# Bilinear pair products on one core: weight loads of eight pairs instead of four, and field 0 held in a store tile

## The chip, the cores and the metric

The kernel runs on one core of a Trainium2 chip. A core has five engines that run their own instruction streams: TensorE (PE) multiplies matrices, VectorE (DVE), ScalarE (ACT) and GpSimd (POOL) work element by element, SyncE (SP) here does nothing but issue DMAs. Sixteen DMA engines move the data between HBM and the on-chip memory (SBUF). The metric is device time in microseconds; the median of repeated runs counts.

## What is computed

The input holds 1024 samples of 32 fields with 128 numbers each; there is one 128 x 128 matrix for each of the 496 pairs of fields (i, j) with i < j. For each pair, field i goes through the pair's matrix, and the result is multiplied with field j element by element:

```python
v_i = inputs[:, I_IDX, :]                 # (1024, 496, 128)
v_j = inputs[:, J_IDX, :]
transformed = jnp.einsum('bpd,ped->bpe', v_i, W)   # W: (496, 128, 128)
return transformed * v_j                  # (1024, 496, 128), float32
```

The output alone is 260 MB; weights are 32.5 MB and fields 16.8 MB.

## The kernel before

Everything is transposed so that the 128 numbers of a field lie across the 128 partitions and the 1024 samples along the row. The pairs are walked from the highest i down, so that few fields are needed at the start: (30,31), (29,30), (29,31), (28,29) and so on. The unit of work, `u`, is half a pair (512 samples).

Sizes and pools, with what each slot costs in a partition's row:

```python
BT, HB = 1024, 512
WC = 2        # pairs per weight split
WL = 4        # pairs per weight load
OG = 2        # pairs per store
NATIVE = 5    # the first five fields go through PE as plain float32
LAG, WLEAD, XLEAD = 3, 4, 3
...
xpool = tile_pool(name="x", bufs=1)    # one tile of 4 KB for each of the 32 fields
spool = tile_pool(name="xs", bufs=2)   # split fields
rpool = tile_pool(name="wr", bufs=5)   # weights as loaded, WL * 512 B
wpool = tile_pool(name="ws", bufs=4)   # split weights
opool = tile_pool(name="o", bufs=4)    # store tiles, OG * 4 KB
ppool = tile_pool(name="ps", bufs=8)   # PSUM, one bank for each u
```

The loads. A weight load brings WL pairs; a row of it is WL * 512 B, one packet for each partition. On the host the weights are laid out so that each load is one contiguous block. All these DMAs, and the stores, go through the queue of SP, which takes them in order and waits there for whatever a DMA needs.

```python
def load_w(c, splits=(0, WL)):
    w_raw[c] = rpool.tile([P, WL, P], F32, tag="w")
    for a, b in zip(splits, splits[1:]):
        nc.sync.dma_start(out=w_raw[c][:, a:b, :], in_=wt[c, :, a:b, :])
```

After the first 15 pairs, PE works on split operands: ACT makes a rounded high part of each weight and each field, POOL the low part and a difference, and three fast matmuls with a scaling in between take the place of one slow float32 matmul.

```python
def split_w(c):                       # two pairs at once
    nc.scalar.mul(h, raw, 1.0 - 2.0**-13)
    nc.gpsimd.tensor_tensor(l, raw, h, ALU.subtract)
    nc.gpsimd.tensor_scalar(d, h, EPS, 1.0, ALU.mult, ALU.mult)
    nc.gpsimd.tensor_tensor(d, l, d, ALU.subtract)

def split_x(f, a):                    # half a field
    nc.scalar.mul(h, x_sb[f][:, s], 1.0 - 2.0**-13)
    nc.gpsimd.tensor_tensor(l, x_sb[f][:, s], h, ALU.subtract)
    nc.gpsimd.tensor_scalar(l, l, 1.0 / EPS, 1.0, ALU.mult, ALU.mult)
    nc.gpsimd.tensor_tensor(d, h, l, ALU.subtract)
```

A field is split when the one before it in the walk begins, half by half. Field 0 is only ever the left field of a pair: after its split nobody reads it.

```python
def first(u):                         # cut: the plain matmul of the first 15 pairs
    po[u] = ppool.tile([P, HB], F32)
    for t in (0, 1):
        nc.tensor.matmul(po[u], w_s[c][t][:, r], x_s[i][t][:, s], start=t == 0, stop=t == 1)
    nc.scalar.mul(po[u], po[u], 1.0 + EPS)

def second(u):
    nc.tensor.matmul(po[u], w_s[c][2][:, r], x_s[i][2][:, s], start=False, stop=True)
    if k == 0 and h == 0:
        ots[g] = opool.tile([P, OG, BT], F32, tag="ot")
    nc.vector.tensor_tensor(ots[g][:, k, s], po.pop(u), x_sb[j][:, s], ALU.mult)
    if k == OG - 1 and h == 1:        # cut: the last two pairs go out in quarters
        nc.sync.dma_start(out=out[g], in_=ots[g])
```

The walk:

```python
load_w(0, (0, 1, WL)); ...fields 30, 31, 29, 28; load_w(1); fields 27, 26; load_w(2); load_w(3)

for u in range(2 * NQ + LAG):
    q = u // 2
    if u % (2 * WL) == 0 and (q // WL + WLEAD) * WL < NQ:
        load_w(q // WL + WLEAD)
    if u < 2 * NQ:
        i, j = pairs[q]
        if u % 2 == 0 and j == i + 1 and 0 <= i - 2 - XLEAD:
            load_x(i - 2 - XLEAD)
        first(u)
    if u >= LAG:
        second(u - LAG)
    if u % 2 == 1:
        ...one of the splits that are due
```

Of the kernel before, what the change touches and what calls it, by code (L numbers as in the profile page):

```python
# [1 line left out]

# [4 lines left out]

F32 = mybir.dt.float32
F32R = mybir.dt.float32r
ALU = mybir.AluOpType  # L10

P = 128
NF = 32
NQ = NF * (NF - 1) // 2
BT = 1024
HB = 512
WC = 2
WL = 4
OG = 2
EPS = 2.0**-12  # L20
NATIVE = 5
LAG = 3
WLEAD = 4
XLEAD = 3


def _pairs():

    return [(i, j) for i in range(NF - 2, -1, -1) for j in range(i + 1, NF)]


@with_exitstack
def kernel(
    ctx: ExitStack,
    tc: tile.TileContext,
    xt: bass.AP,
    wt: bass.AP,
    out: bass.AP,
):

    nc = tc.nc
    pairs = _pairs()
    nchunk = NQ // WC

    xpool = ctx.enter_context(tc.tile_pool(name="x", bufs=1))  # L60
    spool = ctx.enter_context(tc.tile_pool(name="xs", bufs=2))
    rpool = ctx.enter_context(tc.tile_pool(name="wr", bufs=5))
    wpool = ctx.enter_context(tc.tile_pool(name="ws", bufs=4))
    opool = ctx.enter_context(tc.tile_pool(name="o", bufs=4))
    ppool = ctx.enter_context(tc.tile_pool(name="ps", bufs=8, space=bass.MemoryType.PSUM))

    x_sb = {}

    def load_x(f, n=1, pieces=1, eng=None):

        t = xpool.tile([P, n, BT], F32, tag=f"x{f}", name=f"x_{f}")
        s = BT // pieces
        for k in range(pieces):
            (eng or nc.sync).dma_start(out=t[:, :, k * s : (k + 1) * s], in_=xt[:, f : f + n, k * s : (k + 1) * s])  # L74
        for k in range(n):
            x_sb[f + k] = t[:, k, :]

    w_raw = {}

    def load_w(c, splits=(0, WL)):  # L80
        w_raw[c] = rpool.tile([P, WL, P], F32, tag="w", name=f"w_{c}")
        for a, b in zip(splits, splits[1:]):
            nc.sync.dma_start(out=w_raw[c][:, a:b, :], in_=wt[c, :, a:b, :])

    w_s = {}

    def split_w(c):

        k = c * WC % WL
        raw = w_raw[c * WC // WL][:, k : k + WC, :].rearrange("p q e -> p (q e)")  # L90
        h, l, d = [wpool.tile([P, WC * P], F32R, tag=t, name=f"{t}_{c}") for t in ("wh", "wl", "wd")]
        nc.scalar.mul(h, raw, 1.0 - 2.0**-13)  # L92
        nc.gpsimd.tensor_tensor(l, raw, h.bitcast(F32), ALU.subtract)  # L93
        nc.gpsimd.tensor_scalar(d, h.bitcast(F32), EPS, 1.0, ALU.mult, ALU.mult)  # L94
        nc.gpsimd.tensor_tensor(d, l.bitcast(F32), d.bitcast(F32), ALU.subtract)  # L95
        w_s[c] = (h, l, d)

    x_s = {}

    def split_x(f, a):  # L100

        if a == 0:
            x_s[f] = [spool.tile([P, BT], F32R, tag=t, name=f"{t}_{f}") for t in ("xh", "xl", "xd")]
        s = slice(a, a + HB)
        h, l, d = [t[:, s] for t in x_s[f]]
        nc.scalar.mul(h, x_sb[f][:, s], 1.0 - 2.0**-13)  # L106
        nc.gpsimd.tensor_tensor(l, x_sb[f][:, s], h.bitcast(F32), ALU.subtract)  # L107
        nc.gpsimd.tensor_scalar(l, l.bitcast(F32), 1.0 / EPS, 1.0, ALU.mult, ALU.mult)  # L108
        nc.gpsimd.tensor_tensor(d, h.bitcast(F32), l.bitcast(F32), ALU.subtract)  # L109

    nq0 = NATIVE * (NATIVE + 1) // 2
    c0 = nq0 // WC
    first_q = {i: q for q, (i, j) in reversed(list(enumerate(pairs)))}

    todo = []
    for c in range(c0, nchunk):
        todo.append(((c - 3) * WC + 1, max(c * WC, nq0), lambda c=c: split_w(c)))
    for i in range(NF - 2 - NATIVE, -1, -1):  # L120
        for a in range(0, BT, HB):
            todo.append((first_q[i + 1] + 1 if i < NF - 3 - NATIVE else 2, first_q[i], lambda i=i, a=a: split_x(i, a)))
    todo.sort(key=lambda t: t[1])

    load_w(0, (0, 1, WL))
    load_x(NF - 2, pieces=2, eng=nc.scalar)
    load_x(NF - 1, pieces=2, eng=nc.scalar)
    load_x(NF - 3)
    load_x(NF - 4)
    load_w(1)  # L130
    for f in range(NF - 5, NF - 4 - XLEAD, -1):
        load_x(f)
    load_w(2)
    load_w(3)


    ctx.enter_context(tc.manual_schedule())
    po, ots = {}, {}


    def first(u):
        q, h = divmod(u, 2)
        i, c = pairs[q][0], q // WC
        r = slice(q % WC * P, (q % WC + 1) * P)
        s = slice(h * HB, (h + 1) * HB)
        po[u] = ppool.tile([P, HB], F32, tag="po", name=f"po_{u}")
        if q < nq0:
            nc.tensor.matmul(po[u], w_raw[q // WL][:, q % WL, :], x_sb[i][:, s], start=True, stop=True)  # L148
        else:
# [5 lines that stand above are left out]
        q, h = divmod(u, 2)  # L155
        i, j = pairs[q]
        r = slice(q % WC * P, (q % WC + 1) * P)
        s = slice(h * HB, (h + 1) * HB)
        if q >= nq0:
            nc.tensor.matmul(  # L160
                po[u], w_s[q // WC][2][:, r], x_s[i][2][:, s], start=False, stop=True, skip_group_check=True
            )
        g, k = divmod(q, OG)
        if k == 0 and h == 0:
            ots[g] = opool.tile([P, OG, BT], F32, tag="ot", name=f"ot_{g}")
        nc.vector.tensor_tensor(ots[g][:, k, s], po.pop(u), x_sb[j][:, s], ALU.mult)  # L166
        if q >= NQ - 2:
            nc.sync.dma_start(out=out[g, :, k, s], in_=ots[g][:, k, s])
        elif k == OG - 1 and h == 1:
# [5 lines that stand above are left out]
            load_w(q // WL + WLEAD)  # L175
        if u < 2 * NQ:
            i, j = pairs[q]
            if u % 2 == 0 and j == i + 1 and 0 <= i - 2 - XLEAD:
                load_x(i - 2 - XLEAD)
            first(u)  # L180
        if u >= LAG:
            second(u - LAG)
        if u % 2 == 1:
            ready = [t for t in todo if t[0] <= q]
            if ready:
                ready[0][2]()
                todo.remove(ready[0])
    assert not todo


# [25 lines left out]
```

## Time and profile before

| | |
|---|---|
| time, median of 3 | 770.79 us (769.37 to 772.43) |
| span of the profiled execution | 769.2 us |
| PE, DVE, ACT, POOL busy | 93%, 81%, 82%, 80% |
| DMA | 310.11 MB, mean 403 GB/s |
| stores | 247 of 1024 KB, 8.9 us from issue to landing |
| weight loads | 123 of 256 KB and the first in two pieces, 9.1 us to landing |
| field loads | 30 of 512 KB and 4 of 256 KB |

How to read the profile: the page gives each engine's busy time and, in 40 slices of the span, tenths of it that were busy (9 is 90% or more); the row DMA is the mean of the sixteen DMA engines. Groups of instructions are named by line, engine and tile, written out<-in. A wait "DVE ot L166 <- DMA out_dram<-ot: 71.9, 84, 3.3" says that DVE, at its line 166, stood idle 71.9 us in total, 84 times, at most 3.3 us, until a store had landed. SPq is the DMA-issuing queue of SP. A store tile can be written again once its store has landed. Busy shares add up over stages with different limits, so a stage is read by itself.

### The profile page before, as it was taken

How to read it: one execution, taken by the hardware profiler on the slowest of the kernel's cores; microseconds unless marked ns; L12 is line 12 of the kernel's file. 1: busy time of each engine (PE TensorE's matmuls, PEld its weight loads, DVE VectorE, ACT ScalarE, POOL GpSimd, SP SyncE). 2: the span in 40 equal slices, each digit the busy share in tenths (PEclk: the TensorE clock that was granted, in tenths of full speed). 3: DMA queues.
4: the chain of work that ended last, by engine and by line, in shares of the span. 5: the costliest groups of instructions: out<-in, count | busy, mean ns of one | idle time of the engine just before them, and what ended most of it. 6: DMA issues, size and time to landing. Idle time of an engine off the chain costs nothing.

```text
span 769.2 us, 11797 instructions
## 1 busy us (share of the span) xinstructions
PE 715.0 (93%) x2946; PEld 548.9 (71%) x2946; DVE 625.3 (81%) x992; ACT 633.9 (82%) x1256; POOL 611.6 (80%) x883
## 2 busy tenths in 40 slices
PE   7989879889999898999998999999999999999994
PEld 3566657778777686776776877777777777777773
DVE  4767788888988787887787988888888888888885
ACT  2278878888888898898888989898889898998983
POOL 1988998998989878778778697878787869697660
PEclk9999999999999999999999999999999999999997
DMA  9899998999999999999999999999999999999997
GB/s 357 369 411 420 421 400 345 417 410 380 414 422 405 403 395 421 395 416 411 401 420 415 406 414 418 419 415 418 402 419 409 410 410 407 411 413 402 401 399 307
DMA packets 59108, 310.11 MB, mean 403 GB/s; under 512 B 6560, under 2 KB 6816, under 8 KB 27424
## 3 DMA queue, kind: packets, MB, share of 16 engines
q1 hardware_dynamic: 58464, 308.31, 98.8%
q10 hardware_dynamic: 576, 1.05, 0.4%
q8 instruction: 24, 0.39, 0.2%
q14 instruction: 44, 0.36, 0.1%
HBM read 49.28 MB, written 260.05 MB: 402 GB/s over the span
## 4 chain that ended last, share of the span: by engine, by line
PE 49%; DMA 32%; DVE 11%; POOL 6%; issue 1%; DVEq 0%; SPq 0%; ACT 0%; POOLq 0%
DMA out_dram<-ot 31%; PE po L151 31%; PE po L160 15%; DVE ot L166 11%; PE po L148 4%; POOL xd L109 2%; POOL wl L93 1%; POOL xl L107 1%; POOL wd L95 1%; POOL xl L108 0%; DMA x<-in_xt_dram 0%; POOL wd L94 0%; DVEq L166 0%; SPq L74 0%; ACT xh L106 0%
## 5 line engine op out<-in xcount | busy, mean ns | idle before, releaser
L166 DVE TENSOR_TENSOR ot<-po,x 128x512 f32<-128x512 f32 x992 | 625.3, 685 | 135.5 <-DMA out_dram<-ot 71.9
L152 ACT ACTIVATE po<-po 128x512 f32<-128x512 f32 x962 | 549.7, 583 | 109.7 <-PE po L151 61.4
L151 PE MATMUL po<-xh,wh 128*128 128x512 f32 x962 | 387.0, 402 | 25.0 <-DVE ot L166 23.9
L151 PE MATMUL po<-xl,wl 128*128 128x512 f32 x962 | 380.0, 395 | 14.6 <-POOL wl L93 14.1
L160 PE MATMUL po<-xd,wd 128*128 128x512 f32 x962 | 377.3, 393 | 0.0
L151 PEld LDWEIGHTS po<-xh,wh 128*128 128x128 f32 x962 | 181.5, 189 | 96.8 <-DVE ot L166 58.4
L93 POOL TENSOR_TENSOR wl<-w,wh 128x256 fp32r<-128x256 f32 x241 | 177.8, 738 | 74.2 <-ACT wh L92 74.2
L151 PEld LDWEIGHTS po<-xl,wl 128*128 128x128 f32 x962 | 181.9, 189 | 53.9 <-POOL wl L93 19.7
L160 PEld LDWEIGHTS po<-xd,wd 128*128 128x128 f32 x962 | 182.0, 189 | 39.0 <-ACT po L152 0.4
L95 POOL TENSOR_TENSOR wd<-wl,wd 128x256 fp32r<-128x256 f32 x241 | 177.8, 738 | 20.1
L94 POOL TENSOR_SCALAR wd<-wh 128x256 fp32r<-128x256 f32 x241 | 97.4, 404 | 20.3
L92 ACT ACTIVATE wh<-w 128x256 fp32r<-128x256 f32 x241 | 99.0, 412 | 0.0
L107 POOL TENSOR_TENSOR xl<-x,xh 128x512 fp32r<-128x512 f32 x52 | 67.2, 1292 | 17.0 <-ACT xh L106 17.0
L109 POOL TENSOR_TENSOR xd<-xh,xl 128x512 fp32r<-128x512 f32 x52 | 67.0, 1288 | 4.3
L106 ACT ACTIVATE xh<-x 128x512 fp32r<-128x512 f32 x52 | 32.5, 629 | 11.9 <-DMA x<-in_xt_dram 11.7
L108 POOL TENSOR_SCALAR xl<-xl 128x512 fp32r<-128x512 f32 x52 | 32.2, 620 | 4.6
L148 PE MATMUL po<-x,w 128*128 128x512 f32 x60 | 28.9, 647 | 3.9 <-DMA x<-in_xt_dram 3.9
L148 PEld LDWEIGHTS po<-x,w 128*128 128x128 f32 x60 | 12.3, 207 | 19.7 <-issue 15.1
L106 ACT ACT_TABLE_LOAD x1 | 1.3, 1283 | 2.6 <-issue 2.6
L203 POOL MEMSET const-float32-0.0<- 128x1 f32 x1 | 0.1, 98 | 0.2 <-issue 0.2
L203 POOL MEMSET const-bfloat16-1.0<- 128x1 bf16 x1 | 0.1, 101 | 0.0
L203 POOL MEMSET const-uint8-127<- 128x1 uint8 x1 | 0.1, 101 | 0.0
(1 smaller groups left out, 0.1 us busy)
## 6 DMA issues: line engine op xcount, KB each, us to landing
out_dram<-ot SPq DMA_DIRECT2D x247, 1024.0 KB, 8.9
w<-in_wt_dram SPq DMA_DIRECT2D x123, 256.0 KB, 9.1
x<-in_xt_dram SPq DMA_DIRECT2D x30, 512.0 KB, 9.2
x<-in_xt_dram ACTq DMA_DIRECT2D x4, 256.0 KB, 4.9
out_dram<-ot SPq DMA_DIRECT2D x4, 256.0 KB, 7.0
w<-in_wt_dram SPq DMA_DIRECT2D x1, 192.0 KB, 3.5
w<-in_wt_dram SPq DMA_DIRECT2D x1, 64.0 KB, 2.9
```

The costliest lines, as they stand in the source:

```text
L92: nc.scalar.mul(h, raw, 1.0 - 2.0**-13)
L93: nc.gpsimd.tensor_tensor(l, raw, h.bitcast(F32), ALU.subtract)
L94: nc.gpsimd.tensor_scalar(d, h.bitcast(F32), EPS, 1.0, ALU.mult, ALU.mult)
L95: nc.gpsimd.tensor_tensor(d, l.bitcast(F32), d.bitcast(F32), ALU.subtract)
L106: nc.scalar.mul(h, x_sb[f][:, s], 1.0 - 2.0**-13)
L107: nc.gpsimd.tensor_tensor(l, x_sb[f][:, s], h.bitcast(F32), ALU.subtract)
L109: nc.gpsimd.tensor_tensor(d, h.bitcast(F32), l.bitcast(F32), ALU.subtract)
L148: nc.tensor.matmul(po[u], w_raw[q // WL][:, q % WL, :], x_sb[i][:, s], start=True, stop=True)
L151: nc.tensor.matmul(po[u], w_s[c][t][:, r], x_s[i][t][:, s], start=t == 0, stop=t == 1)
L152: nc.scalar.mul(po[u], po[u], 1.0 + EPS)
L160: nc.tensor.matmul(po[u], w_s[q // WC][2][:, r], x_s[i][2][:, s], start=False, stop=True, skip_group_check=True)
L166: nc.vector.tensor_tensor(ots[g][:, k, s], po.pop(u), x_sb[j][:, s], ALU.mult)
```

## The change

A weight load brings eight pairs instead of four: half as many loads, and rows of 4 KB instead of 2 KB. Three buffers take the place of five, and the lead is two loads instead of four, the same sixteen pairs. The weight buffers grow from 5 x 2 KB to 3 x 4 KB in a partition. To make that room, field 0 loses its own tile of 4 KB: it is loaded late, six pairs before field 1 begins, into one of the four store tiles, and this tile goes back to the stores when field 0 has been split.

```diff
-WL = 4
+WL = 8
-WLEAD = 4
+WLEAD = 2
...
-    rpool = ctx.enter_context(tc.tile_pool(name="wr", bufs=5))
+    rpool = ctx.enter_context(tc.tile_pool(name="wr", bufs=3))
...
     def load_x(f, n=1, pieces=1, eng=None):
-        t = xpool.tile([P, n, BT], F32, tag=f"x{f}", name=f"x_{f}")
+        if f == 0:
+            t = opool.tile([P, OG, BT], F32, tag="ot", name="x_0")[:, :n, :]
+        else:
+            t = xpool.tile([P, n, BT], F32, tag=f"x{f}", name=f"x_{f}")
...
     for f in range(NF - 5, NF - 4 - XLEAD, -1):
         load_x(f)
-    load_w(2)
-    load_w(3)
...
-            if u % 2 == 0 and j == i + 1 and 0 <= i - 2 - XLEAD:
+            if u % 2 == 0 and j == i + 1 and 0 < i - 2 - XLEAD:
                 load_x(i - 2 - XLEAD)
+            if u == 2 * (first_q[1] - 6):
+                load_x(0)
             first(u)
```

Here `first_q[1]` is the place of the first pair of field 1, 435 of 496.

## The prediction

> **What bounds the kernel now.** I read the page from its slices down. The DMA row comes first, because the kernel moves 310 MB in 769 us.
>
> ```profile
> PE   7989879889999898999998999999999999999994
> POOL 1988998998989878778778697878787869697660
> DMA  9899998999999999999999999999999999999997
> DMA packets 59108, 310.11 MB, mean 403 GB/s; under 512 B 6560, under 2 KB 6816, under 8 KB 27424
> q1 hardware_dynamic: 58464, 308.31, 98.8%
> ```
>
> The 16 DMA engines are full in nearly every slice. PE shows nines too, but the windows (columns: PE, PEld, DVE, ACT, POOL busy, TensorE clock, DMA share, GB/s) show that it only follows:
>
> ```profile
> 16.00:120.00 104.00, 92.72 (x344) 65.68 (x343) 77.01 (x119) 70.54 (x144) 94.75 (x125) 0.97 0.98 399
> 120.00:240.00 120.00, 112.52 (x481) 90.40 (x479) 103.25 (x157) 105.02 (x213) 108.66 (x152) 0.99 1.00 404
> 240.00:480.00 240.00, 225.86 (x957) 176.25 (x958) 198.10 (x321) 208.29 (x415) 196.59 (x288) 1.00 1.01 409
> 480.00:740.00 260.00, 253.28 (x1069) 196.93 (x1069) 220.96 (x357) 232.32 (x457) 203.15 (x304) 1.00 1.01 411
> ```
>
> From 240 us on DMA is at its limit, while POOL is busy 203 of 260 us and DVE 221. A group of two pairs costs DVE 4 x 685 = 2.7 us; it arrives every 769/248 = 3.1 us. In the first stage POOL is busy 94.75 of 104 us (what is left is mostly the 0.05 to 0.08 us between its instructions): every new field brings a split, and the fields are still short. There, two things are near their limit at once.
>
> The waits say the same for the late stage (300 to 700 us):
>
> ```profile
> DVE ot L166 <- DMA out_dram<-ot: 43.8, 54, 2.5
> PEld po L151 <- DVE ot L166: 35.9, 69, 2.4
> PEld po L151 <- POOL wl L93: 3.6, 4, 0.9
> ```
>
> DVE waits for a store tile until its old store has landed; PE waits for DVE; hardly anyone waits for POOL. So from about 120 us on, a nanosecond of DMA time saved is saved, and a microsecond in which the DMA engines run dry is lost.
>
> **What one packet costs.** The trace records each DMA packet with size and duration. Grouped by size (median and mean ns):
>
> ```
> semaphore, 4 B    x6561    9    9
> weights, 2 KB    x16768   84   86   (1024 of them are pieces of fields 30, 31 and of the last stores)
> fields, 4 KB      x3840  159  173
> stores, 8 KB     x31666  309  317
> ```
>
> The medians lie on a line: 9 ns plus 75 ns for each 2 KB. All packets together take 12.25 million ns, 766 us on each of 16 engines, which is the span.
>
> **What the skill says.** "DMA: Bandwidth & Descriptors", section "Why small descriptors are slow (HBM only)", names a fixed overhead for each packet on the engine's internal bus and fixed metadata for each descriptor. The trace agrees in kind, with 9 ns; it is small beside 84. The same page, "Anatomy of one DMA — SWDGE (gpsimd) path", says that DMA engines don't wait on semaphores: the issuing sequencer does. That matters for the new wait below: SP's queue shows it, with 462.6 us of waiting for DVE ahead of stores. "Perfetto Trace Analysis", section "Identifying the Most-Contended Engine", warns that matmul busy time misleads about headroom. Agreed here: PE's 93% goes with 0.75 us of idle DVE in every 5.8 us around 660 us.
>
> **The change, part by part.**
>
> 1. *Weight packets.* Before, one load of four pairs puts 8 packets and one semaphore on each DMA engine: 8 x 84 + 9 = 681 ns, two loads 1362. After, one load of eight pairs is 8 x 159 + 9 = 1281. Saved: 81 ns for eight pairs, 62 x 81 = 5.0 us if everything counts. Loads issued before 120 us serve the stage in which POOL is as full as DMA. Pair 70 is then at work and loads run 16 pairs ahead, so those from pair 88 on count: 408/8 = 51 loads, 51 x 81 = 4.1 us. The mean of the fields' packets (173) is far over their median; those rows lie 128 KB apart in HBM, while a weight load is one contiguous block as before. I take the weights' excess as before, 2 to 5 ns, and book **-4.0 us**.
>
> 2. *Start.* Loads ahead of field 25 now hold 24 pairs of weights instead of 20: 256 KB more at about 410 GB/s is 0.6 us, less 0.2 for the better packets. POOL's chain begins when field 25 has landed and ACT has split it:
>
> ```profile
> ACT xh L106 <- DMA x<-in_xt_dram: 11.7, 1, 11.7
> POOL xl L107 <- ACT xh L106: 17.0, 3, 15.9
> ```
>
> After that POOL has no gap worth naming until 240 us (under 5 us in all between 17 and 240 us). **+0.4 us.**
>
> There is also something to win. At 25 us the SP queue stands still 8.8 us, because load w_7 waits for a weight split on POOL while two stores stand behind it; DMA runs dry for 1.7 + 0.8 us at 33.5 to 36.1 us.
>
> ```profile
> SPq L83 <- POOL wl L93: 8.8, 1, 8.8
> ```
>
> In the changed program the load in that place waits for PE alone, and the next one waits for an earlier split. That fills the hole. But a full POOL follows until after 100 us, where its results are ready only 1.6 us before DVE needs them, so I book 0.
>
> 3. *Field 0 in a store tile.* The load of field 0 now stands before pair 429. In the built program it takes the tile of store group 210, and from there three tiles rotate instead of four. The first DVE product of group 218 gets that tile back, and its wait is for POOL: for the subtraction that reads the second half of field 0. I replayed this on the times of before (DVE's start of a group, landings at 2.6 us per store and 0.6 per weight load, a store landing some 9 us after issue in the queue).
> With three tiles, groups 214 to 217 start each when a store lands, some 2.5 to 4 us apart; the queue behind them gets short but doesn't run dry. DVE is done with 217 at about 678.8 (before: 675.6). The two halves of field 0's split and the weight split between them take POOL 3.3 + 2.0 + 1.3 us until the last read of field 0, and POOL can begin about 677.0: end at 683.6. In the trace of before the same read ended at 680.48, 4.9 us after DVE had begun group 218 (675.58). So DVE stands still 4.9 us, then writes for 2.5, and the first packet of that store comes about 1.2 us after its issue (as after the hole at 34 us): 687.4. Store 217, the last one queued, is through at 683.7. DMA is dry for 3.7 us and cannot win that back. **+3.7 us** (2 to 5.5).
>
> 4. *Everything else:* the same matmuls, scalings and products, the same bytes. 62 fewer issues on SP, which is not the bound. A weight load now holds the queue for 1.28 us at a time instead of 0.68, which DVE sees as jitter and DMA not at all: 0.
>
> Sum: -4.0 + 0.4 + 0 + 3.7 = +0.1 us. What I left at 0 in step 2 can only be a gain, up to 2.5 us, so I go a little below the sum: **770.0 us** (770.8 before).
>
> **Rivals.**
> - *All saving, no new wait:* the 5.0 us count in full, the hole at 34 us closes (2.5), and the reuse of field 0's tile hides behind queued stores: about 763.5. For it: the DMA row is full from the third slice on. Against it: 3 to 4 us of dry DMA follow from the program's own wait, and POOL leaves no gap early.
> - *4 KB weight packets are no better than two of 2 KB:* if they behave as the fields' do on average, 173 against 2 x 86, only 62 x 9 ns = 0.6 us of semaphores remain, and with field 0 it makes about 774. For it: the mean. Against it: in most slices the fields' median is exactly 159, and their slow ones come in bursts.
> - *A late weight load:* WLEAD 2 x 8 is the same 16 pairs as 4 x 4, some 50 us, against a landing of about 9. A load now brings pairs in lumps, and three buffers must be free in turn, but the reuse distance stays the same (the block before the current one). Little for it; it would add some 1 us stops on SP, as 124 loads already do today, and move the time by less than 1 us.
>
> **Range and chances.** Step 1 may be off by 1.5 us, step 2 by 2.5 downwards, step 3 by 2 either way; the three runs of before spread over 3 us by themselves (769.37 to 772.43), and short drops of the TensorE clock (three before 180 us) are followed by 1 to 3 us of dry DMA each. Range 765.5 to 774.0. A step of 2% would be 15 us; no part here is worth that. Faster by over 2%: 0.01; within 2%: 0.98; slower by over 2%: 0.01.
>
> **What would show it.** Step 1: weight packets with a median near 159 ns, 61 loads of 512 KB beside the first, cut one, and about 50,200 packets in all (59,108 less 7,936 rows and 992 semaphores). Step 2: POOL's first split at 16.8 us instead of 16.35; no SP stop of 8.8 us. Step 3: a DVE wait of about 5 us ended by POOL's subtraction in the field split, once, near 680 us, with GB/s down in that slice and DMA idle for 3 to 4 us. I am wrong if DVE's wait there is there but DMA never runs dry, if the 4 KB weight packets cost 170 or more, or if the early stage shortens by more than 1 us.

## The result, and the profile after

The changed kernel takes 779.76 us (median of six runs, 777.36 to 782.16) beside 770.96 us before (769.37 to 772.43): a ratio of 1.0113, 95% interval 1.0090 to 1.0136. It is 8.8 us slower, where 0.8 us faster was predicted, and it lies outside the predicted range.

The slices of the changed kernel's page, to be laid beside those of before:

```profile
PE   7999788899997999899898989899999999879995
...
PEclk9999999999999999999999999999999999989998
DMA  9999999999999999999999999999999999979998
GB/s 359 421 416 417 401 357 404 402 402 384 419 421 378 386 421 418 387 402 416 401 399 400 404 409 398 388 406 416 409 411 417 411 416 417 374 289 408 423 421 338
DMA packets 50179, 310.10 MB, mean 399 GB/s; under 512 B 5568, under 2 KB 5696, under 8 KB 18496
```

The rates of the kernel before:

```profile
GB/s 357 369 411 420 421 400 345 417 410 380 414 422 405 403 395 421 395 416 411 401 420 415 406 414 418 419 415 418 402 419 409 410 410 407 411 413 402 401 399 307
```

There are 50,179 packets, as counted beforehand (about 50,200), and the same bytes. But the mean rate fell from 403 to 399 GB/s. One place leaps to the eye: slices 35 and 36, 374 and 289 GB/s, the second with a 7 in the DMA row and an 8 in PEclk. The rest is less conspicuous. The DMA row is full everywhere else. The rate is far above that of before in slices 2 and 7 (421 for 369, 404 for 345), below it in 21 to 27 (388 to 409, for 406 to 420), and elsewhere now above and now below.

The stretches (columns as in the prediction: PE, PEld, DVE, ACT, POOL busy, TensorE clock, DMA share, GB/s). First the changed kernel:

```profile
16.00:120.00 104.00, 94.04 (x354) 66.21 (x353) 80.63 (x123) 73.40 (x148) 95.37 (x126) 0.98 1.00 403
120.00:240.00 120.00, 110.56 (x471) 88.55 (x469) 100.80 (x153) 103.27 (x210) 109.85 (x154) 0.99 1.01 406
240.00:480.00 240.00, 223.68 (x942) 175.52 (x943) 196.75 (x317) 204.49 (x406) 191.59 (x281) 0.99 1.00 402
480.00:660.00 180.00, 172.83 (x744) 137.87 (x743) 151.94 (x248) 160.88 (x321) 146.74 (x217) 1.00 1.01 409
660.00:700.00 40.00, 32.20 (x125) 25.63 (x124) 27.46 (x45) 26.94 (x54) 25.57 (x37) 0.87 0.86 334
672.00:676.00 4.00, 4.00 (x12) 3.17 (x11) 2.65 (x5) 2.43 (x5) 0.73 (x1) 0.58 0.87 320
686.00:693.00 7.00, 5.09 (x13) 4.04 (x14) 5.07 (x8) 1.91 (x4) 4.85 (x6) 0.54 0.40 138
```

And those of the kernel before that the prediction did not show:

```profile
480.00:660.00 180.00, 174.56 (x739) 136.17 (x739) 152.94 (x247) 160.69 (x318) 145.18 (x215) 1.00 1.01 412
660.00:700.00 40.00, 39.48 (x167) 30.58 (x166) 34.25 (x57) 36.18 (x72) 32.39 (x48) 1.00 1.01 411
```

From 240 to 660 us the DMA share is 1.00 in both, yet the rate is 402 and 409 instead of 409 and 412 GB/s. Full engines with cheaper packets ought to have moved more. These two traces alone don't tie the lower rate to the rows, though: from 240 to 480 us e1, e3 and e7, kernels with four pairs per load that follow below, moved 406, 402 and 403 GB/s. From 660 to 700 us 77 GB/s are missing: 40 us x 77 = 3.1 MB, or 7.5 us at 410 GB/s. Part of that comes back before the end: DVE begins store group 222 at 11.4 us after its time of before, and its last product 8.2 us after.

DVE's products in that stretch (start, busy time, count, and in brackets the idle time before them with what ended it):

```profile
658.13 7.40 DVE L168 TENSOR_TENSOR ot<-po,x 128x512 f32<-128x512 f32 x12 [1.22 <-DMA out_dram<-ot]
669.69 5.10 DVE L168 TENSOR_TENSOR ot<-po,x 128x512 f32<-128x512 f32 x8 [4.16 <-DMA out_dram<-ot]
676.14 2.49 DVE L168 TENSOR_TENSOR ot<-po,x 128x512 f32<-128x512 f32 x4 [1.35 <-DMA out_dram<-ot]
678.98 2.48 DVE L168 TENSOR_TENSOR ot<-po,x 128x512 f32<-128x512 f32 x4 [0.35 <-PE po L153]
687.16 4.41 DVE L168 TENSOR_TENSOR ot<-po,x 128x512 f32<-128x512 f32 x7 [5.69 <-POOL xl L111]
```

The wait for POOL's subtraction is there, once, 5.69 us long (predicted 4.9); after it the DMA engines ran dry. From 685.2 us on fewer than half of the sixteen were busy for 5.4 us (predicted 3.7), and in the last 3.1 us of that none was; an engine lost 5.2 us on average. Before it comes a stop of 4.16 us for a store that had not landed, with three tiles in rotation. What follows each stop shows in PE. It stands still for 3.1 and 4.7 us, and its clock is at half speed for 3.4 and 6.8 us (0.58 in the window from 672 us, 0.54 in that from 686 us). The first of these stretches begins 1.5 us after PE has resumed, the second while it still stands still. The Trainium skill, "TensorE: Matmul & The Clock Gate", section "What's actually happening", says that the clock is released by activity and falls to half after an idle window of about 3.4 us. The trace agrees in kind: matmuls went from 0.39 to 0.63 us each between 671.9 and 675.3 us, though the stop before, of 3.1 us, was a little shorter than the page's window.

The sums of waits, those of DVE, POOL and the SP queue that answer to the prediction's lines:

```profile
DVE ot L168 <- DMA out_dram<-ot: 55.9, 43, 5.0
...
DVE ot L168 <- POOL xl L111: 5.7, 1, 5.7
...
POOL xl L111 <- ACT xh L110: 16.6, 1, 16.6
```

```profile
SPq L172 <- DVE ot L168: 558.3, 246, 7.8
SPq L87 <- POOL wd L98: 18.4, 23, 1.1
SPq L87 <- POOL wd L99: 8.0, 7, 1.8
```

POOL's first split stands 0.7 us later (16.6 against 15.9, predicted +0.4). SP's stop of 8.8 us is gone: its waits for POOL are 1.8 us at most.

The packets, from the trace's packet records (median and mean ns):

```
                        before        after
weights          2 KB   84   86       4 KB  159  169
stores           8 KB  309  317.4     8 KB  309  319.8
all packets, per DMA engine    765.8 us      767.8 us
```

The floor of 159 ns is what was booked. But the means lie above the floors by more than before: a weight packet by 10 ns instead of 2, a store packet by 11 instead of 8. Over the whole run the stores' excess alone grew from 16.7 to 21.3 us on each engine. So on the DMA engines the saving of the floors was paid back in slower packets. It recurs: with loads of four pairs the stores' mean was 317.0 to 318.7 ns in the whole kernels of this study, with loads of eight 319.1 to 321.1. But large loads alone are not the reason, for e8 below, with loads of two pairs, had 319.4.

### The profile page after: what moved, and what is told of

It reads as the page before. It is cut to its first block, busy times and chain, and to the rows that moved or that the text cites. A ratio compares the mean times of both kernels' runs of the same rounds, so it can differ in the third digit from the quotient of the medians.

```text
span 776.8 us, 11677 instructions
## 1 busy us (share of the span) xinstructions
PE 712.5 (92%) x2946; PEld 553.8 (71%) x2946; DVE 630.6 (81%) x992; ACT 631.9 (81%) x1256; POOL 612.0 (79%) x883
## 2 busy tenths in 40 slices
DMA packets 50179, 310.10 MB, mean 399 GB/s; under 512 B 5568, under 2 KB 5696, under 8 KB 18496
## 4 chain that ended last, share of the span: by engine, by line
PE 52%; DMA 29%; DVE 9%; POOL 8%; issue 1%; DVEq 0%; ACT 0%; POOLq 0%
PE po L153 32%; DMA out_dram<-ot 29%; PE po L162 15%; DVE ot L168 9%; PE po L150 4%; POOL xd L113 2%; POOL wl L97 2%; POOL xl L111 1%; POOL wd L99 1%; POOL xl L112 1%; POOL wd L98 1%; DMA x<-in_xt_dram 0%; DVEq L168 0%; DVEq L213 0%; ACT wh L96 0%
## 5 line engine op out<-in xcount | busy, mean ns | idle before, releaser
L111 POOL TENSOR_TENSOR xl<-x,xh 128x512 fp32r<-128x512 f32 x52 | 67.2, 1292 | 16.6 <-ACT xh L110 16.6
```

## The experiments

Two theories stood at the start. A: field 0's store tile costs the time, through the wait at group 218 and the short rotation before it. B: the rows cost it, because loads of 512 KB slow the packets down or come in lumps. The recorded expectations carry further letters for later variants; the sentence that carries one says what it expects, and what each run says of A and B is told below it. Every ratio is against the kernel before on the same chip.

### One part alone: e1_x0_store_tile, e2_rows_only, e3_x0_split_pool

e1 is the kernel before with field 0 in a store tile and nothing else:

```diff
-        t = xpool.tile([P, n, BT], F32, tag=f"x{f}", name=f"x_{f}")
+        if f == 0:
+            t = opool.tile([P, OG, BT], F32, tag="ot", name="x_0")[:, :n, :]
+        else:
+            t = xpool.tile([P, n, BT], F32, tag=f"x{f}", name=f"x_{f}")
...
+            if u == 2 * (first_q[1] - 6):
+                load_x(0)
```

> The kernel before with only the second half of the change: field 0 loaded late into a store tile, weights still four pairs per load in 2 KB rows. Theory A (field 0's stay in the store pool makes the loss): DVE waits 5 to 6 us once for POOL's subtraction near 680 us, the DMA engines run dry for 4 to 5 us there, time 776 to 779 us, that is most of the measured +9. Theory B (the weight loads make the loss): DVE's wait is there, but the time is within 2 us of before, 769 to 773.

Measured: 771.64 us, ratio 1.0001 (0.9981 to 1.0021). A's 776 to 779 is missed. The reason stands in the waits of e1:

```profile
DVE ot L169 <- POOL xl L110: 2.3, 1, 2.3
```

The wait is 2.3 us, not 5. In e1's built program the tile goes back to group 219, not to 218 as in the changed kernel: presumably the other loads around it shift the order in which the pool's tiles come free. The run undid more than it was meant to, and so became the first hint of what the wait hangs on.

e2 has the rows alone. Field 0 is loaded late into a tile of the field splits that is free by then, and split later:

```diff
-WL = 4
-WLEAD = 4
+WL = 8
+WLEAD = 2
-    rpool = ctx.enter_context(tc.tile_pool(name="wr", bufs=5))
+    rpool = ctx.enter_context(tc.tile_pool(name="wr", bufs=3))
...
+        x_sb[0] = spool.tile([P, BT], F32, tag="xd", name="x_0")
+        nc.sync.dma_start(out=x_sb[0], in_=xt[:, 0, :])
...
+            if u == 2 * (first_q[1] + 3):
+                load_x0()
```

> The changed kernel with eight pairs per load, but field 0 no longer in a store tile: it is loaded after the start of field 1 into the free tile of field splits and split a little later. Theory A: no stall near 680 us, about 6 us less than the changed kernel, 772 to 775; and since the early hole at 34 us is gone, perhaps as fast as before. Theory B: still 776 to 780. In either case the mean of a 4 KB weight packet should be 165 to 170 ns against a median of 159 if the slow tail belongs to the packet size, 160 to 162 if it was chance.

e3 is its control: field 0 as in e2, weights in loads of four pairs as before.

> Control for the run before it: the kernel before, four pairs per load, with field 0 loaded late into the free tile of field splits. Both theories: same as before, 769 to 773; if it is slower, the way in which field 0 is moved here has a cost of its own that must be taken off the other run.

Measured: e2 773.22 us, 1.0007 (0.9991 to 1.0023); e3 772.11 us, 0.9998 (0.9976 to 1.0019). Rows of 4 KB with no stall at all win nothing: the 4 to 5 us that their packets save are not in the time. Nor do they cost anything that can be told from zero here. B as the whole cause falls. So each part alone, as built here, is free, and the two together cost 8.8 us. But e1 is not quite the second part, since its tile goes back one group later.

### Cutting the loads again: e4_two_dmas

The changed kernel, each load issued as two DMAs of four pairs, so that rows are 2 KB again and all else stays:

```diff
-    def load_w(c, splits=(0, WL)):
+    def load_w(c, splits=(0, WL // 2, WL)):
```

> The changed kernel, field 0 in a store tile, but each load of eight pairs cut into two DMAs of four, so that the packets are 2 KB again while buffers, lead and lumps stay. If the long tail of the 4 KB packets costs time, this is faster than the changed kernel by 1 to 3 us (776 to 779). If packets of 4 KB do save their 9 ns, it is slower by 3 to 5 us (783 to 785).

Measured: 778.78 us, 1.0076 (1.0047 to 1.0105). That is 2.8 us less than the changed kernel by the ratios, but the intervals overlap. Weight packets had a mean of 88 ns and stores of 319.1: the stores stayed nearly as slow (319.8) though the rows were small again. That speaks against row size as what slows them, but does not rule it out: by its time e4 stands beside e7 below (four pairs, the same group, 1.0069) and not beside the changed kernel.

### Which group gets the tile back: e5_after_back219, e6_after_back218, e7_x0_back218

Here the store tiles are four tags handed out by hand, so that it is fixed which group gets field 0's tile:

```diff
+BACK = 219        # e6 and e7: 218
+    free = ["ot0", "ot1", "ot2", "ot3"]
+    kept = []
+    def store_tile(name, g=-1):
+        tag = kept.pop() if g == BACK else free.pop(0)
+        (kept if g < 0 else free).append(tag)
+        return opool.tile([P, OG, BT], F32, tag=tag, name=name)
```

e5 and e6 have loads of eight pairs, e7 has four.

> The changed kernel with the four store tiles handed out by hand, so that field 0's tile goes back to store group 219 instead of 218; nothing else. Theory A2 (it is the one group that gets the tile back too early): DVE's wait for POOL shrinks from 5.7 to 1 to 3 us, the DMA engines are dry for 1 us or less, time 771 to 774, the loss is gone. Theory C (field 0's late load, or three tiles in turn, does the harm whatever group comes back): 778 to 781 as the changed kernel.

> Control: the changed kernel with the tiles handed out by hand in the order that it has anyway (group 218 gets field 0's tile). Both theories: 778 to 781, DVE waits 5 to 6 us for POOL.

> Four pairs per load, field 0 in a store tile, but the tile goes back to group 218 by hand (219 without it, which cost nothing). Theory A2: 777 to 780, DVE waits 5 to 6 us for POOL, DMA dry for 4 to 6 us. Theory D (the loss needs loads of eight pairs beside it): 771 to 774.

Measured: e5 775.98 us, e6 780.14 us, e7 777.64 us. With e1, this makes a table of ratios:

```
                        tile back to 219            tile back to 218
four pairs per load     1.0001 (0.9981-1.0021) e1   1.0069 (1.0047-1.0090) e7
eight pairs per load    1.0040 (1.0021-1.0059) e5   1.0110 (1.0091-1.0130) e6
```

One group earlier costs 0.68% with four pairs and 0.70% with eight: 5.2 and 5.4 us, give or take some 2. It does not hang on the row size. The waits and the windows of e5, then of e6, show the mechanism:

```profile
DVE ot L177 <- POOL xl L120: 2.0, 1, 2.0
```

```profile
686.00:693.00 7.00, 5.92 (x26) 4.92 (x27) 6.67 (x12) 4.99 (x11) 6.49 (x10) 1.00 1.00 365
```

```profile
DVE ot L177 <- POOL xl L120: 6.6, 1, 6.6
```

```profile
686.00:693.00 7.00, 3.58 (x8) 2.81 (x9) 4.29 (x7) 1.16 (x2) 6.20 (x9) 0.58 0.17 69
```

The first product of group 218 stands ahead of the point at which POOL has read the second half of field 0. Back to 219, DVE waits 2.0 us, and in this window PE keeps its clock and the DMA engines stay full (share 1.00). Back to 218, it waits 6.6 us, the clock falls to 0.58 and the DMA share to 0.17. e6 repeats the changed kernel by hand, within its interval. The short rotation does slow its own stretch: in e5 PE still stands still for 3.3 us at 666 us, 3.4 us at half clock follow, and from 660 to 700 us it moves 375 GB/s (before: 411). In e1's total nothing of that shows.

e5 misses its forecast of 771 to 774: the wait shrank as expected, but the loss is not gone. The lower row against the upper: eight pairs cost 0.39% and 0.41% here, about 3 us, while e2 showed 0.07% without the store tile. The difference of the two, 0.3%, is about as large as its own uncertainty. Whether the rows cost 0.5 or 3 us is therefore not settled; that they win nothing is. It would fit both that three tiles in turn cost time beside loads of eight pairs and not beside loads of four; no run tries that.

### The opposite direction: e8_rows_1k

Two pairs per load, rows of 1 KB, same lead of 16 pairs:

```diff
-WL = 4
-WLEAD = 4
+WL = 2
+WLEAD = 8
-    rpool = ctx.enter_context(tc.tile_pool(name="wr", bufs=5))
+    rpool = ctx.enter_context(tc.tile_pool(name="wr", bufs=10))
```

> The kernel before with two pairs per load: 248 loads, rows of 1 KB, ten buffers of half the size, a lead of eight loads, so the same sixteen pairs; field 0 as before. If the 9 ns per packet and per semaphore are paid in full by the time, eight pairs cost four loads of 8 packets at 46.5 ns and a semaphore, 1524 ns instead of 1362, over 62 such groups 10 us more: 779 to 783. If a packet's fixed part is made up for by a shorter tail (as 4 KB packets lost it to a longer one), 771 to 775.

Measured: 777.83 us, 1.0082 (1.0060 to 1.0103), so 6.3 us slower. A 1 KB packet took 46 ns; eight pairs cost 32 x 46 + 4 x 9 = 1508 ns instead of 1362, which over 62 times eight pairs is 9 us. Two thirds of the floor sum arrive in the time, which lies between the two forecasts. Smaller rows cost, larger ones do not pay: the curve is flat just where the change sits. The share of store packets over one and a half times their floor was 1.4% here, 2.0% before and 2.9% after: in the whole kernel it rises with the size of a load. Their mean does not: 319.4 ns here, 317.4 before and 319.8 after.

### Lumps: e9_halves

e2 with each load of eight pairs as two DMAs of 64 partitions, issued four pairs apart; rows stay 4 KB, and a DMA brings 256 KB, as in the kernel before:

```diff
+            r = slice(halves[0] * (P // 2), (halves[0] + 1) * (P // 2))
+            nc.sync.dma_start(out=w_raw[c][r], in_=wt[c, r])
...
-        if u % (2 * WL) == 0 and (q // WL + WLEAD) * WL < NQ:
-            load_w(q // WL + WLEAD)
+        if u % WL == 0 and (q // WL + WLEAD) * WL < NQ:
+            load_w(q // WL + WLEAD, halves=(u // WL % 2,))
```

> Rows of 4 KB, field 0 in the pool of field splits (as in the run with rows alone, 773.2), but each load of eight pairs is cut into two DMAs of 64 partitions, issued four pairs apart: packets stay 4 KB, the lumps are 256 KB again and stores run at most two in a row. If long lumps cause the slow stores, the stores' mean falls back from 320 to 317-318 ns and the time to 767 to 770, faster than both kernels; if the row size causes them, 772 to 775.

Measured: 774.18 us, 1.0025 (1.0013 to 1.0036). No better than e2's 1.0007. The stores' mean fell only from 321.1 to 319.6 ns, and the half loads brought a cost of their own: 4 KB packets (weights and fields) had a mean of 175.9 ns beside 167.8 in e2, which is 5.9 us more on each DMA engine. So smaller lumps did not bring the gain back, but whether lumps eat it stays open.

### The transfers by themselves: m1_dma_4pairs, m2_dma_8pairs, m3_dve_4pairs, m4_dve_8pairs, m5_deep_4pairs, m6_deep_8pairs

These kernels leave computation out, and their times are to be read so. m1 and m2 keep only the transfers: no splits, matmuls or products; stores are sent from four zeroed tiles.

```diff
-            nc.sync.dma_start(out=out[g], in_=ots[g])
+            nc.sync.dma_start(out=out[g], in_=fixed[g % 4])
```

> Only the DMA stream of the kernel before, in its order: all loads, all stores, but no split, matmul or product; the stores write the same four zeroed tiles again and again, so nothing waits for data. Summed packet floors (stores 615.3, weights 84.4, fields 41.0 us) give 741 us plus about 8 us of start and end: 749. With the tails that the packets showed in the whole kernel, 765 to 770.

> The same DMA stream with loads of eight pairs in 4 KB rows. Theory P (4 KB rows really save 9 ns per pair of packets and the semaphores): 5 us less than the stream with four pairs. Theory Q (what the packets save comes back as slower packets, in the loads' own tail and in stores that now run four in a row between loads): within 1.5 us of it, either way.

m3 and m4 put DVE's products back in, from two fields in SBUF with no matrix between, into the four rotating tiles. m5 and m6 are the same with eight tiles:

```diff
+        nc.vector.tensor_tensor(ots[g][:, k, s], x_sb[i][:, s], x_sb[j][:, s], ALU.mult)
...
-    opool = ctx.enter_context(tc.tile_pool(name="o", bufs=4))
+    opool = ctx.enter_context(tc.tile_pool(name="o", bufs=8))    # m5 and m6 alone
```

> The DMA stream of the kernel before, four pairs per load, now with DVE in the loop: it multiplies field i with field j straight from SBUF (the matrices, splits and matmuls are left out) into four store tiles in turn, so a store waits for DVE and DVE for a landed store, as in the whole kernel. Both theories: 766 to 773, at the pace of the DMA stream alone (768.7) or a little over it.

> The same with eight pairs per load in 4 KB rows. Theory R (at most three stores queued ahead, which the four tiles allow, are what eats the saving): within 2.5 us of the run with four pairs, though the stream alone gained 8.4 us. Theory S (PE, ACT and POOL eat it: the split stage early and the pace of the matmuls later): 6 to 10 us less than the run with four pairs.

> The DMA stream with DVE in the loop, four pairs per load, but eight store tiles in turn instead of four (the room of the split tiles, which are left out, is free). Theory R (the short store queue): no faster than with four tiles, 767 to 771, since with 2 KB rows the stream alone also took 768.7.

> The same with eight pairs per load and eight store tiles. Theory R: with a deep queue the saving of the 4 KB rows is back, 759 to 763, as in the stream without DVE (760.3). Theory T (it is DVE's own traffic in SBUF, or real data in place of zeros, and not the depth of the queue): 766 to 770, as with four tiles.

Measured (us, ratio to the whole kernel before with its interval, and a store's time from issue to landing):

```
                    four pairs (m1, m3, m5)            eight pairs (m2, m4, m6)
transfers alone     768.66  0.9958 (0.9941-0.9976) 15.4   760.28  0.9838 (0.9815-0.9862) 17.9
DVE, four tiles     769.41  0.9931 (0.9894-0.9968)  9.2   768.66  0.9939 (0.9920-0.9959)  9.1
DVE, eight tiles    772.57  1.0008 (0.9994-1.0023) 15.5   760.70  0.9860 (0.9833-0.9888) 17.9
```

For the ratio of m3, three of its nine executions (771.6 to 772.7 us) count as slow beside its fastest (760.1 us) and are left out; the quotient of the medians is 0.9963.

In the bare stream eight pairs per load are worth 8.4 us, more than the 5.0 of the floors. But only a part of it is the part that was booked. From m1 to m2 the sum of all packets fell from 766.6 to 757.3 us on each engine: 5.0 of these 9.3 us are the weights' floors, of which slower weight packets (166.5 ns on average) took 2.3 back, and the rest came from stores and fields, whose packets got faster (stores from 319.3 to 316.9 ns). DVE with four tiles takes all of the gain away, with nothing else in the kernel that could wait; eight tiles bring it back. The page of m4, then of m6, shows what differs (DVE's row with its idle time and the releaser, and the issue of stores with its median to landing):

```profile
L112 DVE TENSOR_TENSOR ot<-x,x 128x512 f32<-128x512 f32 x992 | 613.5, 686 | 144.6 <-DMA out_dram<-ot 134.6
...
out_dram<-ot SPq DMA_DIRECT2D x247, 1024.0 KB, 9.1
```

```profile
L112 DVE TENSOR_TENSOR ot<-x,x 128x512 f32<-128x512 f32 x992 | 612.9, 686 | 128.1 <-DMA out_dram<-ot 116.9
...
out_dram<-ot SPq DMA_DIRECT2D x247, 1024.0 KB, 17.9
```

And the DMA row and the rates of m4 beside those of m6:

```profile
DMA  9999999999999999999999999999999999999998
GB/s 356 423 422 423 409 395 399 395 395 410 398 403 418 397 395 423 399 389 421 409 384 410 398 409 396 410 392 409 404 415 414 412 413 408 417 414 415 410 413 328
```

```profile
DMA  9999999999999999999999999999999999999995
GB/s 357 421 418 423 419 415 415 401 418 407 412 416 419 421 405 407 403 409 413 412 408 407 404 412 410 413 411 411 424 421 420 425 420 413 420 412 409 414 421 223
```

Both DMA rows are full, and m4's rates still lie below: 395 to 399 in slices 6 to 9, where m6 has 401 to 418. With four tiles a store is issued only after one has landed, and the queue holds some 9 us of work; with eight it holds 18. A full DMA row does not tell these apart; the packets do: all together they take 764.8 us on each engine in m4 and 757.1 in m6, stores 319.6 and 317.6 ns on average.

### A deep queue in the whole kernel: v5_8pairs_8tiles, v6_8pairs_8tiles, v7_4pairs_8tiles

If the shallow queue is what withholds the rows' gain, more store tiles should release it. Kernels with six tiles came first (v3 with eight pairs, the "first of these three" of the next expectation, and v4 with four); their programs deadlock, and they have no time. For eight tiles there is no room either, so the tiles of fields 1 to 8, which are loaded late, serve as store tiles until then. Field 0 goes where e2 has it.

```diff
+    late = (7, 5, 3, 1)
+    free = ["ot0", "ot1", "ot2", "ot3"] + [f"x{f}" for f in late]
...
+            if u % 2 == 0 and j == i + 1 and i - 3 in late:
+                free.remove(f"x{i - 3}")        # v6 and v7: 16 pairs ahead of this
+                load_x(i - 3, 2)
```

v5 hands a tile over at the field's load; v6 takes it out of the rotation 16 pairs earlier; v7 is v6 with four pairs per load.

> As the first of these three, but the tiles of fields 5 to 8 serve as store tiles as well: eight tiles until about 365 us, then seven, six, five and four. Theory R: as fast as with six tiles or 1 to 3 us faster, 764 to 770. Against it: a weight load now waits behind up to seven stores, some 18 us, and the split needs it after about 17, so ACT may wait for weights and the time rise to 770 to 775.

> Eight pairs per load and up to eight store tiles as in the run before, but each pair of field tiles leaves the rotation sixteen pairs before the fields are loaded into it, so that the load finds its tile's store long landed. The run before was 10.6 us ahead of the kernel before at 389 us and then lost about 4 us at each of the four handovers, with SP waiting up to 12.8 us for a store to land. Theory R: the lead stays, 759 to 766. If the handovers were not the cause: 775 to 781.

> The same store tiles and handovers with four pairs per load. Theory R: 768 to 774, no gain from depth alone, so that the lead of the other run is the rows' gain. If it is as fast as the run with eight pairs, the depth helps by itself and the rows do nothing.

Measured: v5 780.94 us, 1.0118 (1.0095 to 1.0140); v6 777.79 us, 1.0069 (1.0053 to 1.0084); v7 770.63 us, 0.9990 (0.9975 to 1.0006). v5 brought a new wait, in its SP queue:

```profile
SPq L199 <- DVE ot L195: 494.2, 233, 7.9
SPq L83 <- DMA out_dram<-ot: 42.0, 5, 12.8
```

Line 83 is the field load: it waits for the last store out of its tile, up to 12.8 us, and everything behind it in the queue waits too; at three handovers fewer than half of the DMA engines were busy for 4.4, 6.8 and 4.2 us. v6 was meant to remove that, but it fell back after its own field loads all the same (one stands at 396 us). Its windows, then v7's:

```profile
400.00:420.00 20.00, 15.12 (x63) 10.99 (x61) 12.33 (x21) 14.44 (x29) 17.37 (x25) 0.98 1.01 403
420.00:440.00 20.00, 20.00 (x76) 16.26 (x77) 16.45 (x27) 15.27 (x30) 9.46 (x16) 0.85 0.88 352
```

```profile
400.00:420.00 20.00, 18.68 (x81) 14.51 (x80) 15.41 (x25) 16.92 (x35) 16.81 (x26) 1.00 1.01 416
420.00:440.00 20.00, 19.69 (x82) 14.71 (x81) 16.85 (x29) 18.11 (x36) 16.34 (x23) 1.00 1.02 421
```

Halfway through, DVE was 10.6 us ahead of the kernel before in v5, and that looked like the gain; but in v7, with the old rows, it was 13 us ahead. It was work that the extra tiles buffered, not time won. So in the whole kernel the deep queue brought nothing for either row size, and with eight pairs it cost, 0.8% against v7. The shallow queue as the reason in the whole kernel is thus not shown. The handovers and the 1 MB field loads confound the answer; a kernel with eight tiles throughout and no handover does not fit and wasn't tried. No version here beat both kernels.

## Why the prediction was wrong

**Step 1, "book -4.0 us", is the step that failed.** Its floor was right (159 ns, 50,179 packets). Two terms under it were wrong. "I take the weights' excess as before, 2 to 5 ns": it was 10 ns, so that by the means eight pairs cost 8 x 169 + 9 = 1361 ns in place of 2 x (8 x 86 + 9) = 1394, and 62 times that difference is 2 us instead of 5. And "a nanosecond of DMA time saved is saved" left the other packets as they were: the stores' excess grew by 4.6 us on each engine. In the whole kernel the rows are worth between +0.5 us (e2) and about +3 us (e5 less e1), that is 4.5 to 7 us worse than booked. The runs show where the saving goes as far as this: without computation eight pairs are faster by 8.4 us (m1 to m2), and that vanishes once DVE fills four tiles that wait for their own stores (m4), while the DMA row stays full; the means of the packets rise instead. The Trainium skill, "Perfetto Trace Analysis", section "DMA Optimizations", says that going from 2 KB to 4 KB can improve throughput dramatically; no run of the whole kernel shows that here, and the streams with a deep queue gained 1.1 and 1.5% (m1 to m2, m5 to m6). Why packets get slower in the shallow loop is not settled: e4 and e9 were to tell row size from lumps, and neither does.

**Step 2** was nearly right and small. POOL began 0.7 us later for 0.4. The hole at 34 us closed as foreseen: DVE stood 2.3 us ahead of before at group 66 (224 us), and lost that again by 243 us in a wait of 4.97 us for a store. Booking 0 held.

**Step 3** had the right mechanism and too small a size: 3.7 booked, 5.2 to 5.4 measured by e7 and e6, which is at the upper end of the 2 to 5.5 given. The wait was 5.7 for 4.9 us and the dry time 5.4 for 3.7. DVE was done with group 217 at 681.5 us (replayed: 678.8), and POOL began the field's split at 680.6 us (677.0). Two things are missing from the replay: the stop of 4.16 us before it and PE's half clock after each stop. What the clock alone cost was not measured. That the wait hangs on the one group to which the tile returns was in the working, yet not tried for what it implied: that 219 would be free.

**Step 4** booked 0 for larger lumps. e9 and e4 don't measure them cleanly enough to say more.

In sum: rows +3.1 (mean of 0.39% and 0.41%) and the tile's return +5.3 make 8.4 us of the 8.8 measured; with e2's +0.5 for the rows 3 us would stay open. The rival "4 KB packets are no better than two of 2 KB" came closest, and in part by its reason: the weights' median stayed at 159 ns, but their mean of 169 came near that of the fields (173 before). The range was too narrow because steps 1 and 3 both erred on the same side, and step 1 by more than the 1.5 us allowed it.

## What to carry to other kernels

A full DMA row proves that the engines are occupied, not that a cheaper packet becomes time: where compute waits for landed stores, try the saving in the stream with that loop in it before booking it. When a load borrows a tile from a rotating pool, look in the built program at which instruction gets it back, and place that behind the last reader; back to group 218 it cost 0.7% more here than back to 219. A lead halfway through a trace after buffers were added is no gain until it is still there at the end.

## What was not expected of the hardware

- Stops of PE of 3.1 and 4.7 us in the changed kernel were followed by 3.4 and 6.8 us at half clock, so a stop may cost more than its length. Not every stop was: after 2.9 us at 238 us in e5 the clock stayed full.
- The line of packet times holds for 1 KB too (46 ns, e8: 9 ns and 37.5 for the KB).
- The share of slow store packets rose with the size of the weight loads between them: 1.4% with 128 KB, 2.0% with 256 KB, 2.9% with 512 KB in the whole kernel. Their mean did not (319.4, 317.4 and 319.8 ns). In the streams without the other engines it was 2.4 to 3.0% for both 256 and 512 KB, so the load's size alone does not set it.
- Twice the store tiles in the stream with DVE made loads of eight pairs 8.0 us faster (m4 to m6, 6.1 by the ratios) and loads of four pairs 3.2 us slower (m3 to m5).
